# Layer 0 of a four-layer kernel: product 9 with C on VectorE in every chunk, a small projection ahead of step 15's sums, gate and mean further back in norm chunks

## The chip, the core and the metric

The kernel runs on one core of a Trainium2 chip. The metric is the device time of one launch in microseconds (us). Before the change the median of three runs was 6422.57 us (6415.79 to 6423.95). The engines are TensorE (PE in the profile, with its weight loads as PEld), VectorE (DVE), ScalarE (ACT), GpSimd (POOL) and SyncE (SP), which issues the DMAs of this layer.

## The reference

Four layers follow one another on a tensor of 2 x 128 x 64 x 64 in float32. The change touches the first alone. It normalises each token over the 128 channels, and then runs the same selective scan (a "mamba" block) over 4096 tokens in four orders for each of the two images: rows forward and backward, columns forward and backward. Its core, for 256 inner channels and 16 states:

```python
dt = jax.nn.softplus(dt @ W_dt.T + b_dt)
...
dA = jnp.exp(dt[..., None] * A)
dBu = dt[..., None] * Bm[:, :, None, :] * xh[..., None]
...
def step(h, inp):
    dA_t, dBu_t = inp
    h = dA_t * h + dBu_t
    return (h, h)
...
y = jnp.einsum('lbdn,bln->bld', hs, Cm)
y = y + xh * Dp
y = y * jax.nn.silu(z)
return y @ W_out.T
```

`dt`, `Bm` and `Cm` come from one small projection, `x_dbl = xh @ W_xp.T`. The four results are joined by a linear layer and added to x. Layers 1 and 2 are attentions over 4096 positions, layer 3 is a smaller selective scan; they stay as they are.

## The kernel before

**Chunks.** Each of the eight scans (2 images, 2 orders, forward or reversed) is cut into 8 chunks of 512 tokens: 64 chunks, numbered k. `ci` is a chunk's place in the sequence (reversed scans go from 7 to 0). Chunks are called forward or reversed here. The normalisation of tokens of later chunks is spread over 12 chunks as well: k = 0 to 3 and 15 to 22 begin one (`ln`: mean, square, variance), and the chunk behind each of them ends it (`lp`: scale). Chunks with `lp` or `ln` are called norm chunks here; there are 14 with at least one of the two, 12 with `lp` and 12 with `ln`.

**Steps.** A chunk has 16 steps, one for each pair of state group and channel block; each works on 128 x 1024 elements. In step s the program issues, for each engine in this order:

- `s_dbu` (L405, GpSimd): dbu of step s + 2, the product of dt*x with B. There are three buffers.
- `s_scan` (L449, VectorE): the scan h of step s from da, dbu and the state carried from the chunk before (hst). Three buffers.
- `V[s]` on VectorE, then `s_hc` (L459 on GpSimd or L461 on VectorE): the product of h of step s - 1 with C. The steps in `POOL_HC` have it on GpSimd, which reads C from SBUF (`cs`); VectorE reads it from a PSUM bank (`pc`) that TensorE fills with a selector matmul (`s_pc`, L438). Product 9 is on GpSimd but where `ci % 3 == 1`. Then `G[s]`.
- sums `y0` and `s_y` (L465, L472, TensorE): the products of two steps are summed over the states into the PSUM bank y. `pairs` says at which step: three steps after a product on GpSimd, two after one on VectorE.
- `xd_` in step 0 (L329, ScalarE; in chunks with `lp` it stands a little later, in `A[0]`, behind `s_da`, `s_fix` and `s_hst`): it copies the small projection out of PSUM, for B and C of the chunk after next.
- `s_da` (L418, ScalarE): da of step s + 1, an exponential into one of two PSUM buffers; `s_fix` (L433) folds the carried state into dbu's first element; `s_hst` (L454) keeps h's last element.
- `A[s]` on ScalarE, `M[s]` on TensorE: the side work. It prepares the next chunks and finishes the last one: `px`, `x_` (convolution, step 9 on), `xsilu` with the table loads around it (step 13), `pz`, `z_` (gate, forward chunks, steps 6 and 13), `pd` (L324, the small projection, step 15), `pt`, `abs_`, `relu_`, `dtsum`, `dtout` (softplus, steps 0 to 6), `po`, `xo` (output projection of the chunk before, L490, L494 and L499 or L501, steps 2 and 4), and in norm chunks `center`, `sub`, `square`, `var`, `keep` (steps 12 to 15) and `ln`, `exp`, `rows`, `scale`, `mul`, `affine` (steps 3 to 10).
- `yg_` (L479, VectorE): the gate, the product of silu(z) with y. The first half is in step 10, the second in step 1 of the next chunk.
- loads (SyncE) of dt, dt*x, B and C for the next chunk, spread over steps 7 to 15.

The order is written by hand (`tc.manual_schedule`); each engine takes its instructions in the order of issue, and one that waits holds up all behind it. The side work shares one PSUM bank, `misc`: whoever fills it waits until the one before has been read. Also y has one bank: `y0` waits for `yg_`, and `yg_` and `dtout` share the buffer "dt".

## Time and profile before

| | us |
|---|---|
| median of 3 runs | 6422.57 |
| lowest, highest | 6415.79, 6423.95 |
| profiled execution, its time | 6431.21 |
| its span, first to last instruction | 6429.4 |
| PE busy in the span | 5699.0 (89%) |
| DVE busy | 5639.6 (88%) |
| POOL busy | 5391.6 (84%) |
| ACT busy | 4413.5 (69%) |

The profile is of one execution. Busy time is the union of an engine's instructions; a share over the whole span is a mean over four layers with different limits, so the part that the change touches has to be read by itself: by the 40 slices of the page, by the windows view (busy time in given stretches), by the waits view (which instruction sat idle until which other one ended) and by the timeline (start, duration, engine, line, output and inputs, and in brackets the idle time before it and what ended it). In the groups of instructions the columns are line, engine, operation, tiles and shapes, count, then busy us and mean ns of one, then the idle time before them with its releaser. In layer 0 the granted TensorE clock, given as a share of the full one, goes up and down within a chunk; its mean from 57 to 3432 us is 0.86.

### The profile page before, as it was taken

Reading aid. Unit: us, or ns where it says so; the run is one execution under the profiler, and the core shown is the slowest. Engines: PE = TensorE matmul, PEld = TensorE weight load, DVE = VectorE, ACT = ScalarE, POOL = GpSimd, SP = SyncE. Lnnn points to the kernel's source line nnn. Section 1 sums busy time; section 2 is a strip of 40 time slices with the busy share of each in tenths; the row PEclk is TensorE's granted clock in tenths of the full one; section 3 lists DMA queues with packets and bytes.
Section 4 is the critical chain, followed back from the end, with each engine's and each line's share of the span. In section 5 each row is a group of like instructions: output and inputs, shape, how many; then the busy total and the mean of one; then the engine's idle time right before and its main releaser. Section 6 shows DMA issues by size and latency. Waiting matters only on the chain. (4 is left out here: it accounts for less than half of the span.)

```text
span 6429.4 us, 66778 instructions
## 1 busy us (share of the span) xinstructions
PE 5699.0 (89%) x20010; PEld 2783.6 (43%) x20010; DVE 5639.6 (88%) x4502; ACT 4413.5 (69%) x7768; POOL 5391.6 (84%) x2519
## 2 busy tenths in 40 slices
PE   8888888888888888888878999999999999888898
PEld 2222222222222222222225888888888788222221
DVE  7999999999999999999997777777777777899997
ACT  7887778877788877787776566555556665545453
POOL 6999999999999999999996677666766566888886
PEclk8888888888888988888878999999999999799887
DMA  6566666566666666666651000000000000977775
GB/s 182 144 154 168 166 152 149 147 151 151 145 149 150 156 151 152 148 155 157 153 144 42 1 5 3 1 1 1 1 1 1 2 6 7 219 184 176 182 176 123
DMA packets 400478, 700.37 MB, mean 109 GB/s; under 512 B 74089, under 2 KB 76658, under 8 KB 399730
## 3 DMA queue, kind: packets, MB, share of 16 engines
q1 hardware_dynamic: 399232, 694.33, 44.5%
q8 instruction: 157, 2.57, 0.2%
q14 instruction: 207, 1.70, 0.1%
q10 hardware_dynamic: 882, 1.78, 0.1%
HBM read 584.53 MB, written 111.28 MB: 108 GB/s over the span
## 5 line engine op out<-in xcount | busy, mean ns | idle before, releaser
L405 POOL TENSOR_TENSOR dbu<-dus,bs 128x1024 f32<-128x1024 f32 x1024 | 2463.4, 2441 | 116.6 <-DVE h L449 97.2
L449 DVE TENSOR_TENSOR_SCAN h<-da,hst,dbu 128x1024 f32<-128x1024 f32 x896 | 2088.9, 2343 | 109.5 <-ACT hst L454 46.6
L418 ACT ACTIVATE da<-dts,aneg 128x512 f32<-128x512 f32 (+1 forms) x2048 | 1411.5, 689 | 210.3 <-DVE h L449 171.2
L1028 POOL TENSOR_TENSOR sum<-sum,sc 128x1024 f32<-128x1024 f32 x378 | 898.1, 2376 | 397.9 <-ACT sc L1023 392.7
L990 ACT COPY sc<-s 128x512 f32<-128x512 f32 x1024 | 596.9, 585 | 703.2 <-PE s L985 574.9
L985 PE MATMUL s<-q,k 128*128 128x256 f32 x4096 | 1051.9, 380 | 10.3 <-ACT lo L943 5.5
L1040 PE MATMUL av<-sc,v 128*128 128x256 f32 x4096 | 1050.3, 379 | 9.1 <-ACT sc L1023 9.1
L472 PE MATMUL y<-hc,cst 128*32 128x512 f32 x4096 | 744.9, 663 | 274.3 <-DVE hc L461 245.3
L997 DVE TENSOR_TENSOR mx<-mx,s 128x512 f32<-128x512 f32 x896 | 609.8, 681 | 369.8 <-ACT sc L990 362.3
L461 DVE TENSOR_TENSOR hc<-h,pc 128x1024 f32<-128x1024 f32 x728 | 870.9, 1196 | 0.6 <-PE pc L438 0.5
L985 PEld LDWEIGHTS s<-q,k 128*128 128x128 f32 x4096 | 770.9, 190 | 124.5 <-issue 8.3
L1040 PEld LDWEIGHTS av<-sc,v 128*128 128x128 f32 x4096 | 772.1, 190 | 116.2 <-ACT sc L1023 14.4
L459 POOL TENSOR_TENSOR hc<-h,cs 128x1024 f32<-128x1024 f32 x296 | 705.1, 2382 | 1.1 <-issue 1.1
L1434 POOL TENSOR_TENSOR A<-A,D 128x1024 f32<-128x1024 f32 x224 | 526.7, 2370 | 134.3 <-DVE D L1439 100.5
L438 PE MATMUL pc<-xd,sel 16*128 16x512 f32 x1024 | 627.3, 699 | 1.3 <-DVE hc L461 1.3
L1020 DVE TENSOR_TENSOR sc<-sc,pm 128x1024 f32<-128x1024 f32 x512 | 620.7, 1213 | 2.2 <-PE pm L1015 1.7
L1023 ACT ACTIVATE sc<-sc 128x1024 f32<-128x1024 f32 x512 | 543.3, 1061 | 43.6 <-DVE sc L1020 43.4
L472 PEld LDWEIGHTS y<-hc,cst 128*32 128x32 f32 x4096 | 109.5, 112 | 805.6 <-DVE hc L461 418.4
L433 ACT ACTIVATE dbu<-hst,dbu,df 128x1 f32<-128x1 f32 x896 | 338.5, 378 | 100.3 <-POOL dbu L405 77.5
L1451 PE MATMUL q<-xs,room 32*128 32x512 f32 x840 | 287.5, 696 | 64.7 <-DVE A L1457 63.5
L438 PEld LDWEIGHTS pc<-xd,sel 16*128 16x128 f32 x1024 | 164.7, 198 | 377.4 <-issue 332.4
L449 DVE TENSOR_TENSOR_SCAN h<-da,dbu 128x1024 f32<-128x1024 f32 x128 | 290.8, 2281 | 16.0 <-POOL dbu L405 5.9
(317 smaller groups left out, 7841.9 us busy)
## 6 DMA issues: line engine op xcount, KB each, us to landing
dts<-ddt SPq DMA_DIRECT2D x512, 256.0 KB, 5.5
dus<-ddu SPq DMA_DIRECT2D x512, 256.0 KB, 5.1
D<-rows SPq DMA_DIRECT2D x448, 256.0 KB, 6.0
bs<-rows SPq DMA_DIRECT2D x1024, 64.0 KB, 4.9
cs<-rows SPq DMA_DIRECT2D x1024, 64.0 KB, 3.3
ddt<-dt SPq DMA_DIRECT2D x128, 256.0 KB, 2.0
ddu<-dtu SPq DMA_DIRECT2D x128, 256.0 KB, 4.1
dtr<-ddt SPq DMA_DIRECT2D x448, 64.0 KB, 2.1
```

Of the source, the lines that this page charges most:

```text
L405: nc.gpsimd.tensor_mul(t, self.dus[q], _bc(self.bs[g], 1, [P, 2, T]))
L418: act(t[:, i, sl], self.dts[q][:, i, sl], AF.Exp, scale=an[:, g, 2 * q + i : 2 * q + i + 1])
L438: mm(t, lhsT=sel[32:48, 4 * g : 4 * g + 4, :].rearrange("p n d -> p (n d)"), rhs=self.xd[32:48, :], start=True, stop=True)
L449: nc.vector.tensor_tensor_scan(ho, ai, bi, init, ALU.mult, ALU.add)
L459: nc.gpsimd.tensor_mul(t, self.h[u], _bc(self.cs[gq(u)[0]], 1, [P, 2, T]))
L461: nc.vector.tensor_mul(t, self.h[u], _bc(self.pc[u // 2], 1, [P, 2, T]))
L472: mm(self.y[q // 2][r : r + 32, :], lhsT=sum4, rhs=self.hc[u][:, i, :], start=False, stop=(u % 8 >= 6), skip_group_check=True)
L985: mm(p[:, o, :], lhsT=j.k[m // 8][:, m % 8 * P : m % 8 * P + P], rhs=self.q, start=True, stop=True)
L997: nc.vector.tensor_max(self.mx, self.s[0][:, 0:2, :] if u == 1 else self.mx, self.p[u])
L1020: nc.vector.tensor_sub(s, s, _bc(self.pm[:, :], 1, [P, 4, NQ]))
L1028: self.adds.tensor_add(self.sum, self.s[0] if w == 1 else self.sum, self.s[w])
L1040: mm(self.av, lhsT=self.job.v[m // 8][:, m % 8, :], rhs=self.s[u // 2][:, m % 4, :], start=(m == 0), stop=(m == 31))
```

## The change

Four edits in layer 0:

1. Product 9 is taken out of `POOL_HC` with its exception: VectorE makes it in all 64 chunks. `pairs` follows, so that the sums of products 8 and 9 come in step 11 and not 12.
2. In chunks without `ln` the small projection `pd` is no longer in `M[15]`, at the end of step 15, but ahead of that step's `y0` and sums in TensorE's order. In chunks with `ln` it stays in `M[15]`, behind `var` and `keep`.
3. In chunks with `lp` the second half of the gate, `yg_(1)`, is issued at the end of step 2 and not of step 1, and `po`, which reads it, in `M[3]` and not `M[2]`.
4. In chunks with `ln` the subtraction of the mean, `sub` (L217), is in `G[13]` and not `V[13]`: behind the product of step 13 on VectorE and not ahead of it.

```diff
-POOL_HC = (0, 5, 9, 11, 14)
+POOL_HC = (0, 5, 11, 14)
...
-                if u in POOL_HC and not (u == 9 and self.ci % 3 == 1):
+                if u in POOL_HC:
...
-                    M[2], A[4] = old.po, (old.xo,)
+                    M[2 if lp is None else 3], A[4] = old.po, (old.xo,)
...
-                    M[15] = nxt.pd
+                    if ln is not None:
+                        M[15] = nxt.pd
...
-                    M[12], V[13] = ln.center, ln.sub
+                    M[12], G[13] = ln.center, ln.sub
...
+                    if s == 15 and nxt is not None and ln is None:
+                        nxt.pd()
                     if s in (3, 11):
                         c.y0(s // 11)
...
-                    if s == 1 and old is not None:
+                    if s == (1 if lp is None else 2) and old is not None:
                         old.yg_(1)
```

## The prediction

> **What bounds the kernel now.** The change is inside the first layer alone, so the page's slices come first:

> ```profile
> PE   8888888888888888888878999999999999888898
> DVE  7999999999999999999997777777777777899997
> POOL 6999999999999999999996677666766566888886
> ```

> Layer 0 is the first 21 slices; VectorE and GpSimd stand at 9 in all but the first. From the first scan (56.7 us) to the end of the last (3431.3) it takes 3374.5 us, 52.7 us for each of 64 chunks. The windows view of four chunks in a row (span, then PE, PEld, DVE, ACT, POOL busy, then the granted clock) shows who is full:

> ```profile
> 3010.72:3060.70 49.98, 41.74 (x123) 12.16 (x122) 49.76 (x32) 35.75 (x66) 49.15 (x23) 0.93 0.68 162
> 3060.70:3111.51 50.81, 41.49 (x121) 11.70 (x120) 49.78 (x31) 40.41 (x84) 50.56 (x23) 0.87 0.61 151
> 3111.51:3164.84 53.33, 44.56 (x124) 13.12 (x123) 49.83 (x30) 40.30 (x84) 51.94 (x24) 0.82 0.62 148
> 3164.84:3217.82 52.98, 42.59 (x123) 12.00 (x122) 50.82 (x32) 40.47 (x84) 51.97 (x24) 0.89 0.67 161
> ```

> Chunk 56 has product 9 on VectorE (as chunk 55 had): 49.98 us, VectorE idle for 0.2. Chunks 57 and 58 have it on GpSimd: VectorE needs 49.8 us, GpSimd 51 to 52, and the chunks take 50.8 and 53.3. So both engines are near the bound, and the time over VectorE's work is in waits. The waits view of VectorE for the whole layer lists them (engine, line, releaser: us in all, times, longest):

> ```profile
> DVE h L449 <- ACT hst L454: 46.6, 30, 2.9
> DVE h L449 <- ACT dbu L433: 40.8, 97, 1.0
> DVE h L449 <- POOL hc L459: 23.7, 37, 1.3
> DVE dt L479 <- PE y L472: 14.2, 12, 2.7
> DVE xc L217 <- PE misc L213: 10.6, 10, 2.0
> ```

> With the smaller ones it is 145 us of 3374.5; 3229.4 is work. I went through VectorE's timeline chunk by chunk, adding the idle times, to see at which step each stands: all 30 of the first kind are at step 1, the third at steps 14 and 3, the fourth at step 1 and the fifth at step 13 of norm chunks, the second at steps 15 (18.4 us), 10 (11.7) and 0 (9).

> **The 40 products.** 64 chunks have product 9; 24 (ci 1, 4, 7) are on VectorE already, 40 move.

> ```profile
> L461 DVE TENSOR_TENSOR hc<-h,pc 128x1024 f32<-128x1024 f32 x728 | 870.9, 1196 | 0.6 <-PE pc L438 0.5
> L459 POOL TENSOR_TENSOR hc<-h,cs 128x1024 f32<-128x1024 f32 x296 | 705.1, 2382 | 1.1 <-issue 1.1
> ```

> On VectorE one lasts 1.196 us, but the next scan begins 1.11 us after it (3091.66 to 3092.77 in the timeline), since ends overlap. So +40 x 1.11 = **+44.4** of VectorE's work (47.8 by the full length). All of it is on the path: VectorE has nothing else to hide it. [...] The row speaks for 1.11.

> GpSimd loses 40 x 2.31 us. Its four products (2.31 from start to start), 16 dbu (2.37) and two dtu (1.23) come to 49.6 us, below VectorE's new 50.8. What it made late were the products 11 and 14, whose scan buffers VectorE waits for: 23.7 us, 0.8 at step 14 of most reversed chunks with product 9 on GpSimd and none in chunk 56. Between 0 and 23.7 can go; I take **-23.7**, by chunk 56, and -3 for small waits at steps 3, 7 and 13 behind the same backlog. But a wait of ScalarE stands right behind. In step 13 it loads a table, does two Silu and loads a table again (1.28 + 1.15 + 1.28 us), and only then da(15); in chunks with product 9 on VectorE step 15 waits 0.64 for it (chunks 43, 46, 59), in the others 0.2 because step 14 had waited already. 48 chunks (the 50 without norm work, less the last two, which have no Silu) x 0.64 = 30.7 against 18.4 now: **+12.3** (0 if the other waits keep covering it). The sums of products 8 and 9 come one step earlier on TensorE; behind them are the selector matmul for product 12, due two steps later, and the mean: nothing is late.

> **The small projection.** At the start of chunk 58:

> ```profile
> 3109.07 1.92 PE L472 MATMUL y<-hc,cst 128*32 128x512 f32 x4 [1.56 <-DVE hc L461]
> 3110.93 3.69 PE L324 MATMUL misc<-xs,m 128*73 128x512 f32 x4
> 3114.66 0.68 ACT L329 ACTIVATE xd<-misc,vec 73x512 f32<-73x512 f32 x1 [3.27 <-PE misc L324]
> 3117.45 2.35 DVE L449 TENSOR_TENSOR_SCAN h<-da,hst,dbu 128x1024 f32<-128x1024 f32 x1 [2.50 <-ACT hst L454]
> ```

> TensorE idles until product 13 is made, does its sums, then the projection; ScalarE, in order, stands 3.27 us at xd, and da(1) and the scan of step 1 come 2.50 us late. Ahead of the sums, the projection needs only the Silu (done 3106.17) and TensorE (free at 3107.5): it ends at 3111.2, before ScalarE is there (3111.38). The wait goes in reversed chunks: 34.0 of the 51.2 us at step 1. In forward chunks the bank is also held by the z copy, done at 2694.16 in chunk 49, while the sums let the projection start at 2694.91:

> ```profile
> 2693.59 0.57 ACT L304 COPY sz<-misc 128x512 f32<-128x512 f32 x1
> 2694.91 3.69 PE L324 MATMUL misc<-xs,m 128*73 128x512 f32 x4
> 2701.43 2.35 DVE L449 TENSOR_TENSOR_SCAN h<-da,hst,dbu 128x1024 f32<-128x1024 f32 x1 [1.75 <-ACT hst L454]
> ```

> Only 0.75 us is won per chunk: of 17.2 us in 13 waits, 9.7 go. Together **-43.7** (ends 0 and -51.2). The new wait on that copy holds up the sums of product 13 by up to 5 us, and with them pt(0) and the sums of 14 and 15: projection to 2697.95, sums 1.92, selector and pt(0) 2.1, sums 1.06, so near 2703; VectorE's gate stands behind a scan that then ends at 2702.9. The slot of product 12, wanted by GpSimd at 2701.77, is free at 2699.9. 0 to 3 us; I take 0.

> TensorE had 0.71 of its clock from 3100 to 3112; the projection took 3.69 us there and 1.94 at 3059.30. [...]

> **Gate and mean in 12 norm chunks.**

> ```profile
> 1106.94 0.69 DVE L217 TENSOR_TENSOR xc<-x,misc 128x512 f32<-128x512 f32 x1 [1.31 <-PE misc L213]
> 1121.67 0.69 DVE L479 TENSOR_TENSOR dt<-sz,y 128x512 f32<-128x512 f32 x1 [1.10 <-PE y L472]
> ```

> Behind product 12 (1.11 us) the subtraction, and behind the next scan and product the gate (3.4 us), find their data. 14.2 + 10.6 = 24.8 us. The gate's output sums move from step 2 to 3, behind y0 and two sums (2.1 us): at half clock (4.7 us) in this chunk they would end near 1131.9, and ScalarE, which came for them at 1130.88, waits up to 1.6 us; at full clock nothing. 0 to 20 us; I take 5: **-20** net (ends 0 and -24.8). Nothing that is moved issues a DMA, and SP's and GpSimd's orders are otherwise as before.

> **Sum.** 44.4 - 23.7 - 3 + 12.3 - 43.7 - 20 = **-33.7**. The profiled execution took 6431.2 (span 6429.4); it becomes 6397.5. It lies 8.6 over the median 6422.6, so I predict **6389** for the median. About 0.2% (13 us) is what a measurement of this kernel tells from no change.

> **Rivals.**
> - *More is freed* (0.14). Beside the sum, the rest of step 1 (7.5), of the norm chunks (5), and the 20.7 us at steps 10 and 0 go, and step 15 doesn't grow (12.3): up to -79, 6343. For it: 102.7 of VectorE's 145 us of waits stand where the change reaches. Against: steps 10 and 15 are ScalarE's own table loads.
> - *The projection is not the cause* (0.09). It starts earlier but ScalarE is held elsewhere, so step 1 keeps its 43.7: +10, 6433, no difference. For it: ScalarE waits 148 us for dtsum too (L381). Against: the 3.27 above ends with the projection.
> - *ScalarE sets the pace* (0.11, slower). By its timeline it waits only 1.3 us per chunk for VectorE in forward and norm chunks; if it, held by TensorE at half clock, is what ends steps 1 and 13, the waits come back as waits for da: 44.4 - 23.7 - 3 + 12.3 = +30, 6453. It decides if under 30 of the 63.7 us at step 1 and in norm chunks go. Against: in reversed chunks ScalarE waits 4.2 us for VectorE.

> **Numbers.** The forecast has 0.66, from 6364 (the 7.5, the 5 and the 12.3 go too) to 6409 (the gate's 20 are lost). 6345 to 6418 leaves out the slower case, half the third and a little below: 0.8. Faster 0.66 + 0.14 = 0.80, same 0.09, slower 0.11.

> **What would show it.** After: x256 of L459 and x768 of L461; step-1 waits of VectorE below 15 us in all, POOL hc below 5, the two norm rows below 6, ACT dbu near 50. L324 ahead of the step's sums, xd's 105.2 us of waiting (the waits view of ScalarE) below 40. Layer 0 ends near 3398. Wrong if VectorE's waits stay over 100 us in the layer: then ScalarE holds it. A new wait at L501 or L479 would be the price of the moved gate.

## The result and the profile after

The change is slower. Median 6441.75 us (6437.61 to 6461.23) against 6417.76 (6410.89 to 6423.95) for the kernel before, six runs each: ratio 1.0044, 95% interval 1.0028 to 1.0061. Predicted were 6389 (6345 to 6418). The profiled execution took 6437.8, with a span of 6436.0.

The page shows the work that moved: the 40 products are on VectorE (x728 to x768, x296 to x256), each as long as before.

```profile
DVE  7899999999999999999998777777777777899998
POOL 6899998899999999999996676666766666788887
L461 DVE TENSOR_TENSOR hc<-h,pc 128x1024 f32<-128x1024 f32 x768 | 917.2, 1194 | 3.7 <-PE pc L438 3.5
L459 POOL TENSOR_TENSOR hc<-h,cs 128x1024 f32<-128x1024 f32 x256 | 606.4, 2369 | 7.3 <-PE y L472 5.3
```

VectorE is at 9 in one slice fewer of layer 0, and GpSimd has three slices of 8. Layer 0 takes 3394.2 us from the first scan to the end of the last, against 3374.5: 19.7 more, near the 24 of the medians. The windows view of the same four chunks (56 to 59):

```profile
3039.11:3089.08 49.97, 44.57 (x122) 12.31 (x122) 49.75 (x31) 35.35 (x66) 48.45 (x23) 0.86 0.65 154
3089.08:3140.44 51.36, 45.55 (x122) 12.86 (x122) 50.73 (x32) 40.66 (x85) 50.38 (x23) 0.80 0.66 161
3140.44:3192.76 52.32, 46.07 (x122) 13.19 (x122) 50.83 (x32) 40.38 (x85) 50.71 (x23) 0.80 0.63 156
3192.76:3244.12 51.36, 44.13 (x122) 12.57 (x122) 50.73 (x32) 40.67 (x85) 48.81 (x23) 0.87 0.62 151
```

These reversed chunks did what was forecast: VectorE 50.7 us busy of 51.4 in two of them (50.8 of 52.3 in the third), GpSimd below it, 205.0 us for the four against 207.1. The loss is elsewhere. Adding up the chunks by kind, scan to scan (14 norm chunks, 19 other forward ones, 31 other reversed ones): norm 755.8 before and **792.0** after, forward 999.0 and 1003.7, reversed 1619.8 and 1598.5. The waits view of VectorE for the layer says what it waits for now:

```profile
DVE h L449 <- ACT dbu L433: 81.2, 118, 3.1
DVE h L449 <- ACT hst L454: 29.1, 32, 1.2
DVE h L449 <- POOL hc L459: 1.2, 1, 1.2
```

GpSimd's 23.7 us are gone (1.2), and so are the rows of the gate (14.2) and the mean (10.6). But the row of dbu (L433, an instruction of ScalarE behind da) has doubled from 40.8 to 81.2, and its longest wait has gone from 1.0 to 3.1: VectorE waits for ScalarE. ScalarE's own waits, in the same stretch:

```profile
ACT da L418 <- DVE h L449: 232.6, 270, 2.4
ACT xd L329 <- PE misc L324: 71.5, 35, 3.7
ACT x L501 <- PE misc L494: 20.2, 17, 2.5
ACT r L231 <- PE misc L226: 6.7, 6, 1.8
```

The second and third of these rows before the change:

```profile
ACT xd L329 <- PE misc L324: 105.2, 54, 3.8
ACT x L501 <- PE misc L494: 4.4, 12, 0.8
```

The projection's row fell from 105.2 to 71.5, but not below the 40 that was forecast: in reversed chunks it nearly went, in norm chunks it rose from 23.3 to 35.3. The third row is the one that grew: 20.2 us at the copy of the output sums, 13 of them in chunks 18 to 23, 2.1 to 2.5 in each. The chunks 21 and 22 of both kernels, first after, then before (windows view):

```profile
1201.52:1259.54 58.02, 50.40 (x142) 15.01 (x140) 52.64 (x33) 47.28 (x100) 50.05 (x23) 0.82 0.56 137
1259.54:1317.57 58.03, 50.41 (x142) 15.00 (x140) 52.65 (x33) 47.28 (x100) 50.04 (x23) 0.82 0.55 137
```

```profile
1169.64:1224.22 54.58, 47.58 (x142) 14.19 (x138) 51.31 (x32) 47.35 (x100) 52.07 (x24) 0.84 0.59 145
1224.22:1278.82 54.60, 47.59 (x142) 14.20 (x138) 51.31 (x32) 47.33 (x100) 52.02 (x24) 0.84 0.57 144
```

VectorE has 1.3 us more work in each (the product), yet the chunk is 3.4 longer, and now no engine is full: VectorE idles 5.4 of 58.0. That is a ring of waits, in which each engine stands for another in turn, and not an engine's work. The timeline of chunk 20, which begins at 1143.49, shows a part of it (start, duration):

```profile
1150.89 2.35 DVE L449 TENSOR_TENSOR_SCAN h<-da,hst,dbu 128x1024 f32<-128x1024 f32 x1 [1.68 <-ACT dbu L433]
1154.27 0.68 DVE L479 TENSOR_TENSOR dt<-sz,y 128x512 f32<-128x512 f32 x1
1155.00 2.07 PE L465 MATMUL y<-xs,diag_d 128*128 128x512 f32 x2 [1.91 <-DVE dt L479]
1158.62 1.96 PE L490 MATMUL misc<-x,cst 128*128 128x512 f32 x2
1160.41 1.90 PE L494 MATMUL misc<-dt,wof 128*128 128x512 f32 x4
1162.34 1.04 ACT L501 COPY x<-misc 128x512 f32<-128x512 f32 x1 [2.12 <-PE misc L494]
1172.22 2.35 DVE L449 TENSOR_TENSOR_SCAN h<-da,hst,dbu 128x1024 f32<-128x1024 f32 x1 [1.06 <-ACT hst L454]
```

The gate waits for nothing now, but nothing is won by it: the scan of step 2 begins 7.4 us into chunk 20 in both kernels. Before, the gate's wait stood ahead of it; now it waits for da, since ScalarE's copy of the projection, ahead of da in its order, waits 2.78 us for TensorE (1.61 before). And `y0`, in order on TensorE, waits 1.91 for it (y has one bank), runs at half clock (0.50 granted from 1155.00 to 1157.10; its two matmuls take 2.07, and 1.02 at 1129.71 in the kernel before), the output sums come behind, and ScalarE, which reached L501 at 1160.22, stands 2.12 there. What is queued behind it on ScalarE is that much later, and at step 8 the scan waits 1.06 for ScalarE.

### The profile page after: what moved, and what is told of

The parts are those of the page before. It is cut to its first block, busy times and chain, and to the rows that moved or that the text cites. A ratio compares the mean times of both kernels' runs of the same rounds, so it can differ in the third digit from the quotient of the medians.

```text
span 6436.0 us, 66790 instructions
## 1 busy us (share of the span) xinstructions
PE 5731.6 (89%) x20010; PEld 2789.9 (43%) x20010; DVE 5675.5 (88%) x4542; ACT 4416.4 (69%) x7768; POOL 5303.6 (82%) x2479
## 3 DMA queue, kind: packets, MB, share of 16 engines
q1 hardware_dynamic: 399232, 694.33, 44.4%
## 4 chain that ended last, share of the span: by engine, by line
PE 42%; DVE 15%; issue 14%; ACT 11%; POOL 10%; DMA 7%; SPq 2%; DVEq 0%; ACTq 0%; POOLq 0%
PE s L988 13%; PE av L1043 13%; DVE h L449 7%; POOL dbu L405 5%; ACT da L418 4%; DVE hc L461 3%; DMA D<-rows 3%; PE y L472 2%; DVE D L1442 2%; POOL A L1437 2%; PE misc L285 2%; PE misc L324 2%; PE misc L375 1%; PE misc L1103 1%; DMA dus<-ddu 1%
## 5 line engine op out<-in xcount | busy, mean ns | idle before, releaser
L449 DVE TENSOR_TENSOR_SCAN h<-da,hst,dbu 128x1024 f32<-128x1024 f32 x896 | 2086.8, 2341 | 111.4 <-ACT dbu L433 81.2
L461 DVE TENSOR_TENSOR hc<-h,pc 128x1024 f32<-128x1024 f32 x768 | 917.2, 1194 | 3.7 <-PE pc L438 3.5
L472 PE MATMUL y<-hc,cst 128*32 128x512 f32 x4096 | 770.6, 690 | 162.4 <-DVE hc L461 157.9
L438 PE MATMUL pc<-xd,sel 16*128 16x512 f32 x1024 | 618.0, 694 | 1.3 <-DVE hc L461 1.3
L459 POOL TENSOR_TENSOR hc<-h,cs 128x1024 f32<-128x1024 f32 x256 | 606.4, 2369 | 7.3 <-PE y L472 5.3
L472 PEld LDWEIGHTS y<-hc,cst 128*32 128x32 f32 x4096 | 108.9, 115 | 724.1 <-DVE hc L461 315.8
L433 ACT ACTIVATE dbu<-hst,dbu,df 128x1 f32<-128x1 f32 x896 | 337.5, 377 | 51.4 <-POOL dbu L405 30.0
L438 PEld LDWEIGHTS pc<-xd,sel 16*128 16x128 f32 x1024 | 166.6, 198 | 371.8 <-issue 341.4
L449 DVE TENSOR_TENSOR_SCAN h<-da,dbu 128x1024 f32<-128x1024 f32 x128 | 290.4, 2278 | 13.9 <-POOL dbu L405 5.6
```

What stands on the lines that cost most here:

```text
L438: mm(t, lhsT=sel[32:48, 4 * g : 4 * g + 4, :].rearrange("p n d -> p (n d)"), rhs=self.xd[32:48, :], start=True, stop=True)
L449: nc.vector.tensor_tensor_scan(ho, ai, bi, init, ALU.mult, ALU.add)
L461: nc.vector.tensor_mul(t, self.h[u], _bc(self.pc[u // 2], 1, [P, 2, T]))
L472: mm(self.y[q // 2][r : r + 32, :], lhsT=sum4, rhs=self.hc[u][:, i, :], start=False, stop=(u % 8 >= 6), skip_group_check=True)
```

## The experiments

Theory after the result: ScalarE, held by TensorE, sets the pace of norm chunks, and edits 3 and 4 hand it its data later (the prediction's third rival, in norm chunks). Rival: product 9's work on VectorE is the loss. All times are scan to scan in the profiled execution; ratios are to the kernel before, with 95% intervals. "Sums late" means that the sums of products 8 and 9 stay in step 12.

| kernel | edits | ratio | norm | forward | reversed |
|---|---|---|---|---|---|
| before | | 1 | 755.8 | 999.0 | 1619.8 |
| the change | 1 2 3 4 | 1.0044 [1.0028, 1.0061] | 792.0 | 1003.7 | 1598.5 |
| no_gate_move | 1 2 4 | 1.0036 [1.0022, 1.0050] | 786.8 | 1004.9 | 1595.5 |
| no_mean_move | 1 2 3 | 1.0032 [1.0019, 1.0046] | 787.4 | 1005.3 | 1597.6 |
| products_and_projection | 1 2 | 0.9998 [0.9987, 1.0009] | 764.9 | 1004.7 | 1595.9 |
| no_product9 | 2 3 4 | 1.0024 [1.0012, 1.0036] | 777.0 | 999.2 | 1600.9 |
| only_projection | 2 | 0.9976 [0.9965, 0.9987] | 753.9 | 997.8 | 1595.8 |
| only_product9 | 1 | 1.0058 [1.0039, 1.0076] | 767.6 | 1020.2 | 1605.3 |
| only_gate | 3 | 1.0025 [1.0013, 1.0036] | 776.6 | 996.9 | 1607.2 |
| only_mean | 4 | 1.0007 [0.9996, 1.0018] | 761.7 | 997.8 | 1609.2 |
| projection_and_mean | 2 4 | 0.9980 [0.9967, 0.9993] | 758.1 | 1000.6 | 1600.9 |
| only_output_sums | half of 3 | 0.9989 [0.9977, 1.0001] | 757.3 | 1001.5 | 1613.0 |
| gate_once | 3 in one chunk | 0.9998 [0.9986, 1.0010] | 760.3 | 999.0 | 1619.4 |
| projection_reversed | half of 2 | 0.9965 [0.9952, 0.9978] | 753.9 | 998.0 | 1600.8 |
| projection_z_early | 2, z copy earlier | 0.9961 [0.9946, 0.9975] | 755.8 | 991.7 | 1602.9 |
| sums_of_9_late | 1 2 4, sums late | 0.9974 [0.9964, 0.9985] | 756.2 | 1006.0 | 1593.8 |
| only_product9_sums_late | 1, sums late | 1.0019 [1.0009, 1.0028] | 760.4 | 1018.3 | 1608.5 |
| all_four_sums_late | 1 2 3 4, sums late | 1.0022 [1.0010, 1.0033] | 782.8 | 1004.0 | 1597.5 |
| z_early_products_reversed | 2, z copy earlier, product 9 of reversed chunks on VectorE, sums late | 0.9956 [0.9940, 0.9971] | 755.6 | 992.4 | 1597.6 |
| z_early_products_mean_sums_late | 1 2 4, sums late, z copy earlier | 0.9957 [0.9940, 0.9973] | 756.8 | 988.3 | 1594.9 |

Each class time is of one execution. Reversed chunks that no edit touches took 1607.2 to 1619.8 us (before, `only_gate`, `only_mean`, `only_output_sums`, `gate_once`), so a difference of 13 in that column tells nothing by itself; norm chunks took 753.9 to 755.8 where edit 2 touches two of them at most (before, `only_projection`, `projection_reversed`, `projection_z_early`).

### One edit taken back

Each kernel is the changed one with one edit of the diff reversed; `products_and_projection` has 3 and 4 reversed.

```diff
 no_gate_move
-M[2 if lp is None else 3], A[4] = old.po, (old.xo,)
+M[2], A[4] = old.po, (old.xo,)
...
-if s == (1 if lp is None else 2) and old is not None:
+if s == 1 and old is not None:
 no_mean_move
-M[12], G[13] = ln.center, ln.sub
+M[12], V[13] = ln.center, ln.sub
 no_product9
-POOL_HC = (0, 5, 11, 14)
+POOL_HC = (0, 5, 9, 11, 14)
...
-if u in POOL_HC:
+if u in POOL_HC and not (u == 9 and self.ci % 3 == 1):
```

> The change with edit 3 undone (gate and output sums of norm chunks where they were). Theory G (the later gate holds up y0 and the output sums on TensorE, ScalarE stands at the copy L501 and paces the norm chunks): norm chunks fall from 56.6 to about 54.2 us, L501's wait from 20 us to under 6, the ratio to the kernel before from 1.0044 to 0.998-1.000. Theory V (the 44 us of products on VectorE are simply on the path): ratio stays near 1.004. Theory M (the later mean makes square, variance and the projection late): ratio stays at 1.003 or above.

> The change with edit 4 undone (mean subtracted ahead of the product again). G: norm chunks stay at 56 to 57 us, ratio 1.002-1.005; VectorE waits for L213 again, some 10 us, which costs little since ScalarE paces. V: 1.004. M: L231's wait (6.7 us) goes, xd waits less, norm chunks fall by 2 us, ratio 0.999-1.001.

> Edits 1 and 2 alone. G: norm chunks at 54.0 to 54.8 us, as with edit 3 undone; reversed chunks 51.6 and forward 52.8 as in the whole change; ratio 0.997-1.000. V: 1.004. M: 0.999, and below the kernel that keeps edit 4.

> The change with edit 1 undone (product 9 on GpSimd in 40 chunks again). G: norm chunks stay above 56 us, reversed and forward ones move by under 0.6 us each, ratio 1.002-1.005. V: the whole 44 us come back, ratio 0.996-0.998. M: as G.

Theory G failed in the first of these (norm chunks 56.2 us each and a ratio of 1.0036, where it asked for 54.2 and at most 1.000), theory M in the second (1.0032, where it asked for 1.001 at most). `products_and_projection` came as G has it (54.6 us, 0.9998), and with `no_product9` (1.0024) it excludes theory V, which asked for 1.004 and 0.996 to 0.998.

Taking back the gate or the mean alone gives nearly nothing (norm 786.8 and 787.4); taking back both gives 22 us more. So either is enough for most of the loss beside product 9. Without product 9 the two still cost 21 to 23 us (777.0 against 753.9 and 755.8). In norm chunks the rival (product 9's work) explains at most the difference of 15 between 792.0 and 777.0.

### One edit alone

Each is the kernel before with one edit; `projection_and_mean` has two.

> The kernel before with edit 2 alone. Theory S (edit 2 is the whole gain, in reversed chunks; edits 3 and 4 lengthen a chain between ScalarE and TensorE at the end and start of norm chunks that already set their pace): reversed chunks 1600 us in all (1619.8 before), forward 998 (999.0), norm 755 (755.8), ratio to the kernel before 0.996-0.998. Rival I (the edits hurt and help only in combination): reversed chunks keep their waits, now at step 14 for GpSimd, ratio 0.999-1.000.

> The kernel before with edit 1 alone. S: 44 us of products against some 24 of waits for GpSimd; reversed and forward chunks 5 us longer each, norm chunks 5 to 10 longer, ratio 1.001-1.004. I: step 1 keeps its waits and all 44 us show, 1.005 or more.

> The kernel before with edit 3 alone. S: the copy L501 waits for the output sums (16 us in all, 0.4 now), norm chunks 12 to 22 us longer in all, the rest as before, ratio 1.002-1.004. I: harmless without product 9, norm chunks within 4 us of 755.8, ratio 1.000.

> The kernel before with edit 4 alone. S: VectorE's 10.6 us of waiting for L213 go but the gate waits longer for the sums (14.2 us now, over 25 then), norm chunks 8 to 20 us longer in all, ratio 1.001-1.003. I: harmless without product 9, norm chunks 745 to 756 us, ratio 0.999-1.000.

> Edits 2 and 4, product 9 and gate as before. Theory N (the later mean costs much only where product 9 is on VectorE too, since both push back the chain square, variance, projection): norm chunks 754-764, ratio 0.997-0.999. Rival: the mean costs in norm chunks what it cost beside product 9 (22 us): norm chunks 774-780, ratio 1.000-1.002.

`only_projection` and `only_gate` came as theory S has them, `projection_and_mean` as theory N. `only_product9` did not: 1.0058 is above S's range and in that of rival I. Its forward chunks take 21.2 us more than before, with VectorE's waits at steps 1 and 10 up from 17.2 and 8.7 to 24.3 and 14.3. `only_mean` lies between its two theories.

Edit 2 alone is a gain (0.9976, some 15 us); edits 1 and 3 alone are losses; the mean alone makes no difference that can be told, and beside edit 2 it costs 4 us in norm chunks, not the 22 that it costs beside 1 and 2 (764.9 to 786.8). In `only_mean` VectorE's wait at the mean goes from 10.6 to 2.6, and the one at step 1 of norm chunks rises from 16.3 to 19.0. In `only_gate` the wait at the gate goes, and 13 us each come up at steps 2 and 8, with 1.44 us of waiting of ScalarE at L501 per norm chunk.

`only_projection` also shows why forward chunks (997.8) gained nothing. Its timeline, from the last step of chunk 50 into chunk 51:

```profile
2725.71 0.58 ACT L304 COPY sz<-misc 128x512 f32<-128x512 f32 x1
2726.34 3.69 PE L324 MATMUL misc<-xs,m 128*73 128x512 f32 x4 [3.43 <-ACT sz L304]
2730.07 0.68 ACT L329 ACTIVATE xd<-misc,vec 73x512 f32<-73x512 f32 x1 [1.68 <-PE misc L324]
2732.86 2.35 DVE L449 TENSOR_TENSOR_SCAN h<-da,hst,dbu 128x1024 f32<-128x1024 f32 x1 [1.06 <-ACT hst L454]
```

The projection, now first in the queue, holds TensorE idle for 3.43 us until the z copy is read; then its four matmuls take 3.69 us at half clock (1.94 at full clock), and the scan still waits 1.06. They take 3.29 to 3.69 us in 18 of the 19 forward chunks, and in 7 of 19 before. The granted clock at step 15 of forward chunks is 0.57 here, 0.72 before.

### The gate or the sums behind it

```diff
 only_output_sums (against before)
-M[2], A[4] = old.po, (old.xo,)
+M[2 if lp is None else 3], A[4] = old.po, (old.xo,)
 gate_once (against before)
-M[2], A[4] = old.po, (old.xo,)
+M[3 if k == 18 else 2], A[4] = old.po, (old.xo,)
...
-if s == 1 and old is not None:
+if s == (2 if k == 18 else 1) and old is not None:
```

> Half of edit 3 on the kernel before: the output sums in M[3], the gate still in step 1. Theory X (the sums behind y0 end too late for ScalarE's copy): L501 and L499 wait about 20 us in all as in only_gate, norm chunks 768-778, ratio 1.002-1.003. Rival Y (the later gate holds y0, TensorE idles and slows): L501 and L499 under 8 us, norm chunks 752-762, ratio 0.999-1.001.

Moving the output sums alone costs nothing (norm 757.3; ScalarE waits 4.6 us at L501 in the whole layer). So it is the gate and not the place of `po`. That the gate does it by keeping `y0` from TensorE is read from the timeline of the change (1.91 us at 1155.00).

> Edit 3 in chunk 18 alone, nothing else changed. In all five kernels with the later gate, chunks 19 to 22 take 58.02 to 58.06 us each, 17 times the 3.413 us at whose multiples the granted clock changes in the record; in before and three others they take 54.6, 16 times. Theory R (two stable rhythms): the clock's grid holds a rhythm once it is entered, so one late gate is enough and chunks 19 to 22 stay at 58.0: norm chunks 768 to 777, ratio 1.001 to 1.003. Theory S (each late gate costs its own chunk): chunk 18, perhaps 19, is longer by up to 3.4 us and chunks 20 to 22 are back at 54.6 to 54.8: norm chunks 755 to 761, ratio 0.999 to 1.001.

Theory S, as put for this kernel. Chunk 18 takes 56.5 against 53.9, chunk 19 55.3, chunk 20 55.0, and chunks 21 and 22 are back at 54.6. A late gate costs its own chunk some 2.6 us and dies out in three. Where each of them has one, nothing dies out: all five kernels with the whole of edit 3 take 58.02 to 58.04 us in each of chunks 20 to 22.

### The z copy earlier, and the projection in reversed chunks alone

```diff
 projection_z_early (against only_projection)
-M[13], A[14] = lambda: new.pz(1), (lambda: new.z_(1),)
+m13 = 13 if ln is not None else 12
+M[m13], A[m13 + 1] = lambda: new.pz(1), (lambda: new.z_(1),)
...
-A[13] = (nxt.xsilu, exp_and_ln)
+A[13] = (*A.get(13, ()), nxt.xsilu, exp_and_ln)
 projection_reversed (against only_projection)
-if ln is not None:
+if ln is not None or not new.rev:
     M[15] = nxt.pd
...
-if s == 15 and nxt is not None and ln is None:
+if s == 15 and nxt is not None and ln is None and new.rev:
     nxt.pd()
```

> Edit 2 alone, with the gate matmul and the z copy of forward chunks one step earlier (steps 12 and 13, ahead of the Silu). Theory C (in forward chunks the early projection makes TensorE idle 3.4 us for the z copy, its clock halves, and step 1 waits 1.06 us every time): the gap goes, VectorE's step-1 waits of forward chunks fall from 18 us to under 6, step 15's grow by up to 0.6 each, forward chunks 985-994 us in all (997.8), ratio to the kernel before 0.994-0.997. Rival Q (step 1 waits for ScalarE's own queue of Silu, table loads and copies, whatever TensorE does): step 1 stays at 15-18, ratio 0.997-0.998 or above.

> Edit 2 only where no z copy stands ahead of the projection (next chunk reversed). C: reversed chunks about 1597 as with the whole edit 2, forward ones 996-1000 with uneven waits at step 1 (0 to 2.9) as before the change; ratio 0.997-0.998, the same as edit 2 whole: its forward half wins nothing. Rival of the prediction (0.75 us won per forward chunk): forward chunks 10 us above only_projection, ratio 0.999.

Theory C, in both (the ratio of the second, 0.9965, is a little below the 0.997 that it asked for). With the copy out of the way, the wait at step 1 of forward chunks is under 1 us in all (18.0 in `only_projection`), the clock at step 15 is 0.97, and forward chunks take 991.7; but 23.1 us wait at step 15 for ScalarE. In `projection_reversed` they are as before (998.0), so the forward half of edit 2 wins nothing by itself. Beside edit 1 it may: with the whole of edit 2 forward chunks fall there from 1020.2 to 1004.7, and the halves weren't tried. The two ratios can't be told apart (0.9961, 0.9965).

### Product 9 with its sums where they were

```diff
-pairs.setdefault(max(m + (3 if m in POOL_HC else 2) for m in (u, u + 1)), []).append(u)
+pairs.setdefault(max(m + (3 if m in (*POOL_HC, 9) else 2) for m in (u, u + 1)), []).append(u)
```

> Edits 1, 2 and 4 as in no_gate_move (norm chunks 786.8 us, granted clock at steps 14 and 15 of norm chunks 17 to 22 0.52 and 0.50), but the sums of products 8 and 9 stay in step 12 as before. Theory P: it is the earlier sums that leave TensorE idle in step 12 and 13 and drop its clock, and with the clock the mean's chain is late: the clock at 14 and 15 stays near 1.0, norm chunks come to 765 to 770, ratio 1.000 to 1.002. Theory Q: it is product 9 on VectorE itself (VectorE's own time in step 10, and the later scan 11): the clock stays at 0.5, norm chunks 782 to 790, ratio 1.003 to 1.005.

Theory P, and more of it than was expected (765 to 770): norm chunks 756.2 against 786.8 with this one line, ratio 0.9974 against 1.0036. The timeline from the end of chunk 21 into chunk 22, first of `no_gate_move`:

```profile
1242.56 1.07 PE L472 MATMUL y<-hc,cst 128*32 128x512 f32 x8
1247.34 2.07 PE L298 MATMUL misc<-xnt,m 128*128 128x512 f32 x2 [1.60 <-DVE xc L217]
1253.20 1.87 PE L226 MATMUL misc<-meanw,sq 128*128 128x1 f32 x8
1255.11 0.27 ACT L231 ACTIVATE r<-misc,eps 128x4 f32<-128x4 f32 x1 [1.27 <-PE misc L226]
1256.86 3.69 PE L324 MATMUL misc<-xs,m 128*73 128x512 f32 x4
1260.59 0.68 ACT L329 ACTIVATE xd<-misc,vec 73x512 f32<-73x512 f32 x1 [3.13 <-PE misc L324]
1263.51 0.69 DVE L479 TENSOR_TENSOR dt<-sz,y 128x512 f32<-128x512 f32 x1 [3.68 <-PE y L472]
```

and of `sums_of_9_late`:

```profile
1218.34 1.06 PE L472 MATMUL y<-hc,cst 128*32 128x512 f32 x8
1222.04 1.13 PE L298 MATMUL misc<-xnt,m 128*128 128x512 f32 x2 [1.57 <-DVE xc L217]
1226.50 1.05 PE L226 MATMUL misc<-meanw,sq 128*128 128x1 f32 x8 [1.29 <-ACT sq L221]
1228.44 0.26 ACT L231 ACTIVATE r<-misc,eps 128x4 f32<-128x4 f32 x1
1232.27 0.68 ACT L329 ACTIVATE xd<-misc,vec 73x512 f32<-73x512 f32 x1 [1.48 <-PE misc L324]
1235.19 0.69 DVE L479 TENSOR_TENSOR dt<-sz,y 128x512 f32<-128x512 f32 x1 [0.98 <-PE y L472]
```

Same instructions, same idle time ahead of L298 (1.60 and 1.57). In the first kernel TensorE comes out of it at half clock and stays there: the variance takes 1.87 instead of 1.05, r waits 1.27, xd 3.13, and the gate 3.68. In the second it keeps its clock to the end of the chunk. In chunks 17 to 22 the granted clock at steps 14 and 15 is 0.52 and 0.50 against 1.00 and 1.00. My reason for theory P was wrong in one point: the earlier sums don't make the idle time longer. As I read the traces, they move it against the instants at which the recorded clock changes (last section).

The low clock alone doesn't make the loss. In `products_and_projection`, with the earlier sums but the mean in its old place, the clock at these steps is 0.53 and 0.50 as well, and norm chunks take 764.9; with the later mean but the sums late (`sums_of_9_late`) or as before (`projection_and_mean`, clock 1.00) they take 756.2 and 758.1. The 786.8 need both.

> All four edits, with the sums of products 8 and 9 kept in step 12. Theory P+Y: two separate faults, the earlier sums and the later gate. The sums' part goes (chunks 0 to 4 back from 57.5 to about 54.5, the forward chunks unchanged), the gate's ring of 58.0 us stays in chunks 18 to 22: norm chunks 772 to 780, ratio 0.999 to 1.002. If the gate's price too is due to the low clock that the earlier sums leave (theory P alone): chunks 18 to 22 at 54.5, norm 752 to 758, ratio 0.996 to 0.998.

Two faults, then: chunks 2 to 4 go back from 57.4 to 57.9 in the change to 54.8, 54.6 and 54.1 (chunk 1 stays at 57.2), and the gate keeps chunks 18 to 22 at 58.0. The clock says the same: in the change it is low at step 14 in chunks 1 to 4 (0.62; 0.99 with the late sums) and 1.00 there in chunks 17 to 22. Norm 782.8 is above the 772 to 780 expected. Against `sums_of_9_late` the gate costs 26.6 us in norm chunks and 0.5% in the ratio.

> Edit 1 alone with the sums of products 8 and 9 kept in step 12 (only_product9, 1.0058, has them in step 11). Prediction's own terms for edit 1: +44.4 of VectorE's work, -23.7 of waits for GpSimd, +12.3 at step 15: +33, ratio 1.004 to 1.006. If nearly all that edit 1 cost was the earlier sums: ratio 0.999 to 1.002.

On the edge of the second case: 1.0019 against 1.0058. Alone, edit 1 costs some 12 us, and its earlier sums 25 more by the medians. By class only norm chunks show that (760.4 against 767.6); forward and reversed differ by 2 and 3 us, so the traces of the layer show 6 of the 25 (3387.1 against 3393.2), and the rest isn't explained.

### Versions that beat both kernels

> projection_z_early (0.9961, reversed chunks 1602.9 us, norm 755.8, forward 991.7) with product 9 on VectorE also in all reversed chunks. If VectorE's work is what bounds reversed chunks, some 20 more products of 1.11 us cost 22 and give back the wait at step 14 (about 14): ratio 0.997 to 0.998, reversed 1608 to 1612. If the product takes the place of the wait at no net price there, as products_and_projection against only_projection says (1595.9 and 1595.8): reversed 1595 to 1604, ratio 0.995 to 0.997.

> Edits 1, 2 and 4, sums of products 8 and 9 kept in step 12, and the z copy a step earlier as in projection_z_early; the gate stays in step 1. If the gains add: norm chunks 756 as in sums_of_9_late, forward 992 to 1000 (1006 there, less the step 1 wait), reversed 1594: ratio 0.9945 to 0.996. If the z copy and VectorE's longer forward chunks collide: forward 1003 to 1008, ratio 0.997 to 0.998.

Product 9 on VectorE takes the place of the wait for GpSimd at no net price in reversed chunks (1597.6 against 1602.9; step 14 has no wait left). The last kernel has the shortest layer, 3340.0 us, and the lowest median, 6390.21 us, with the forward chunks at 988.3, below the 992 to 1000 expected if the gains add. Its ratio 0.9957 [0.9940, 0.9973] can't be told from that of `projection_z_early`. With `projection_z_early` these are three kernels faster than the kernel before and the change.

## Why the prediction was wrong, point by point

By class, the prediction's terms and the profile: reversed chunks have 19 of the 40 products (21.1), less 34.0 at step 1, less 18.0 at steps 14, 3 and 7, plus some 10 at step 15, so about -21; measured -21.3. Forward: 12 products (13.3), less 9.7, less 6.8, plus 3, so about 0; measured +4.7. Norm: 9 products (10.0), less 20 and 1.3, so about -11; measured **+36.2**. The miss lies in the norm chunks.

- **Gate and mean, -20 net. This step failed.** The two waits went (14.2 and 10.6 to 0), as said, but the waits for da at steps 2 and 8 came in their place. The prediction took 5 us for the later gate and let ScalarE wait "up to 1.6 us" at L501, then nothing. From the start of `y0` to the end of the output sums it took 7.3 us (1155.00 to 1162.31 in chunk 20) where 2.1 and 4.7 were foreseen for half clock, though the granted clock was 0.50 only up to 1158.30 and 1.00 at L490 and L494; and the wait was 2.1 in each of the settled chunks, and part of it was carried into the next chunk (`gate_once`), since ScalarE has little slack in norm chunks (it waits 1.3 us per chunk for VectorE there): the gate costs 21 us alone and 27 beside the other edits (`only_gate`; `all_four_sums_late` against `sums_of_9_late`). Its upper end, 20, was reached. The mean cost 4 to 6 by itself (761.7 against 755.8, 758.1 against 753.9), and 22 beside the earlier sums.
- **"The sums of products 8 and 9 come one step earlier on TensorE ... nothing is late." This failed too**, and cost 31 us of norm chunks beside edit 4 (`no_gate_move` against `sums_of_9_late`), 9 beside all four (792.0 against 782.8). Nothing is late by the order of the queue; it is late because TensorE drops to half clock there (0.52 granted at step 14 of chunks 17 to 22 in `no_gate_move`, 1.00 in `sums_of_9_late`) and edit 4 brings the mean later. The prediction looked at order and not at clock there.
- **The 40 products, 44.4 less 23.7.** The work is real: VectorE is busy 3268.6 us in the layer, 39.2 more, and the waits for GpSimd went. With the sums kept in step 12, edit 1 costs +12 us alone and nothing beside 2 and 4 (0.9974 against 0.9980), where the terms, with the +12.3 and the -3, give +30. VectorE's waits for others absorb more of the work than was priced. Step 15 waits 0.63 per reversed chunk, as forecast.
- **The small projection, -43.7.** In reversed chunks the wait went as said, 31.9 to 3.8 at step 1. But the term was too large, and that the class agrees (-21 and -21.3) is in part luck: the profiled execution of before was heavy there. In `only_gate` and `only_mean`, whose reversed chunks are unchanged, step 1 waits 17.6 and 19.8 us, in `gate_once` 30.1. Some of the wait also came back behind it: in `only_projection` steps 3 and 15 of reversed chunks rise from 3.0 and 9.4 to 5.4 and 14.7. By the medians the whole of edit 2 is worth 15 us, not 43.7. In forward chunks it failed (17.2 to 15.9, 9.7 predicted): the new wait on the z copy, which the prediction saw and priced at 0 for the sums, left TensorE idle (3.43 us at 2726.34 in `only_projection`), and the projection itself ran at half clock behind it (3.69 us for its four matmuls, 1.94 at full clock).

Most of the 7.5 us that the low end of the forecast's range takes off at step 1 came only with the z copy out of the way (`projection_z_early`, granted clock 0.97 at step 15): forward chunks went from 997.8 to 991.7. In `only_projection` they had not moved (999.0 before).

- **Signs.** It had named VectorE's waits over 100 us in the layer as the sign that ScalarE holds it, and they came to 125.5 (145 before). Step 1 has 21.3 (below 15 forecast), the row of dbu 81.2 (near 50). The waits for GpSimd (1.2) and at gate and mean (0) came as forecast, and so did the wait at L501, which it had named as the price of the moved gate.
- **Rivals.** The third was the nearest: +30, 6453 for 6442. It was placed on all of step 1; it held in norm chunks alone. The argument against it ("in reversed chunks ScalarE waits 4.2 us for VectorE") was true and beside the point, for the edits 3 and 4 are not in reversed chunks.
- **Not settled.** Why edit 3 costs nothing in chunks 2 to 4 of `only_gate` (54.7, 54.6, 54.2, and 53.9, 55.0, 54.2 before) and 3.4 us in chunks 19 to 22. What the gate would cost if TensorE kept its clock wasn't tried. Why edit 1 without edit 2 lengthens forward chunks by 21 us, where its terms give some 10, is open too.

## What to carry to other kernels

Where an engine stood idle at the end of an in-order chain, moving its instruction back took away the wait that the profile showed (14.2 us at the gate), and gave what it produces to the next engine later (20.2 us of ScalarE's waiting at L501, 4.4 before): price that from the engine without slack in that stage (here ScalarE), chunk upon chunk. The matmul group that was put first in TensorE's queue while its bank was still held turned a late sum into an idle TensorE (3.43 us in `only_projection`), and paid in forward chunks when its predecessor moved too (991.7 against 997.8). When a change moves the sums of a step, look at the clock row of the stage (0.52 and 1.00 at step 14 for the same idle time ahead of L298, 1.60 and 1.57), not at the order alone.

## What the runs showed of the hardware

**Settled chunks were multiples of it.** Chunks 21 and 22 take 54.54 to 54.63 us in the kernel before and in ten of the experiments, all without edit 3 but `gate_once`: 16 times 3.413 is 54.61. In the five kernels with the whole of edit 3 they take 58.02 to 58.04, and 17 times is 58.03; they begin at the same place of the grid, within 0.04 us. Four sit on neither: `no_gate_move` (57.72, 57.84), `products_and_projection` (56.09, 54.75), `only_product9` (56.08, 54.77) and `only_output_sums` (54.36, 54.51). That a cause worth little in itself so cost a whole 3.4 us per chunk, and two together little more than one, is how I read these figures. The rhythm did not hold by itself: in `gate_once` chunks 21 and 22 were back at 54.6.

**Unchanged code varies.** Layers 1 to 3, the same in all these kernels, take 2978 to 3006 us from one profiled execution to another, and the kernel before had medians of 6407.85 to 6432.6 beside the experiments. Differences of a few us are read from the chunks and the intervals, not from one execution's total.
